# An attention and feed-forward block: V by seven products, K's and Q's weights together, codes by bits, norms on ScalarE

## Chip, cores and metric

The kernel runs on one core of a Trainium2 chip. The metric is the device time of one execution in microseconds. Times of before: 1510.03, 1510.06 and 1511.17 us, median 1510.06.

The engines are called PE (TensorE matmul), PEld (its weight loads), DVE (VectorE), ACT (ScalarE), POOL (GpSimd) and SP (SyncE, which issues all DMAs here).

## What is computed

16 sequences of 256 tokens, model width 256, 16 heads of 128, feed-forward width 2048. Everything is float32; the feed-forward weights come as 4-bit codes, two to a byte, with one scale for 32 of them.

```python
x = L0_attn_x                                    # (16, 256, 256)
n = layernorm(x)
q, k, v = (einsum('bpd,hde->bphe', n, W) + b for W, b in ((W_Q, b_Q), (W_K, b_K), (W_V, b_V)))
s = where(causal, einsum('bqhe,bkhe->bhqk', q, k) / sqrt(128), -1e5)
z = einsum('bkhe,bhqk->bqhe', v, softmax(s))
x = x + layernorm(einsum('bqhe,hed->bqd', z, W_O) + b_O)
n = layernorm(x).reshape(4096, 256)
Wg, Wu, Wd = (LUT[codes] * scales for each of gate, up, down)    # (2048,256), (2048,256), (256,2048)
x = x + layernorm((gelu(n @ Wg.T) * (n @ Wu.T)) @ Wd.T)
```

## The kernel before

**Three passes for a product.** Matmuls run on float32r operands. A matrix is kept as a high part (`hi`, rounded by a copy on ACT) and a rest (`lo = x - hi`, by a subtraction on DVE or POOL); `mm3` (L352) multiplies hi x hi, hi x lo and lo x hi into one PSUM bank. So a product of 128 x 128 by 128 x 512 is three matmuls, and what one operand costs elsewhere is an ACT copy and a subtraction.

**Attention.** The 4096 tokens are 8 blocks of 512 (two sequences). A unit is one head in one block, 128 units in all; a pair of heads shares the K, Q and output weights, a group of four heads (`w`, 32 groups) shares V's. The main loop (L1023) takes one step per unit and keeps several units in flight. In step `i` it records, in this order: scores and exps of unit i+4 (`st_s`, L421), K and Q of unit i+5 (`st_qk`, L370), the transpose of the probabilities on DVE (`st_t`), the output product of an earlier pair (`st_o`), the split of the turned probabilities (`st_p`), a quarter of V (`st_v`, L402), the product with V of unit i (`st_z`, L492), and the DMAs that write and read back the transposed probabilities through HBM (`hop`, `pt`: `st_w`, `st_b`), which land one and two steps before they are used.

`st_v` makes V for 128 tokens of each of the two sequences and 512 columns: two contraction halves (`kt`) x three passes = 6 matmuls of 512 columns into the bank `pv`; four such calls make a group. The first two are split into `vh` (ACT) and `vl` (DVE, from the bank), the last two are copied to `vr` (ACT), because the last 128 tokens of a sequence meet only the diagonal tile, which is multiplied unsplit in float32.

**Order.** Every engine works through its instructions in the order in which they are recorded; `run` (L95, so nearly all rows of the profile say L99) and `dma` (L86, rows say L91) enforce it. Side jobs are generators in lanes (`splits`, `urgent`, `behind`, `made`, `spare`, `idle`). Each `yield` names the engine of the job's next piece (V_ is DVE, G_ POOL, A_ ACT, N_ none), and `slot(kinds)` (L133), called at fixed places of a step, runs one piece of the first lane whose next piece has that kind.

**Weights.** In the first block `w_raw` (L283) loads raw weights, `w_split` (L297) splits them and `w_keep` writes hi and lo to HBM; from the second block on `w_get` (L331) loads these: K and Q 512 KB each for a pair, three steps before use, V 2 x 512 KB for a group. Each kind has two buffers.

**Norms.** `ln1` (L231) and `mid` (L555) compute means and variances on DVE, the power -1/2 on POOL, and apply them with `ln_apply` (L175) on POOL, four instructions of 128x256 for each norm; only the last block's `mid` does it on ACT (`ln_apply_act`, L183).

**Feed-forward weights.** From the end of the first block on, `f_make` (L618) decodes 24 pieces of codes on DVE: two extractions, a sign, a mask, and four operations that turn the code's three bits into a value with maxima; `f_scale` (L650) multiplies by the scale on POOL, splits, and builds four sums of 128x128 tiles for gate and up.

**Feed-forward.** Gate and up are already made by seven products in place of eight (`Two`, L778 on): with the token halves 11, 21, ... and the weights' sums, `m1` to `m7` are accumulated so that four results come out of seven products (the Winograd form of Strassen's method). `x_ops` (L710) makes the token sums.

Of the kernel before, what the change touches and what calls it, by code (L numbers as in the profile page):

```python
# [13 lines left out]
BF16 = mybir.dt.bfloat16  # L14
# [4 lines left out]
P = 128  # L19
# [9 lines left out]
def kernel(  # L29
# [21 lines left out]
    qscale = -1.0 / math.sqrt(E)  # L51

# [122 lines left out]
    def ln_apply(dst, src, mv, rs, t):  # L175
        run(nc.gpsimd.tensor_scalar, dst, src, mv[:, t, 0:1], rs[:, t : t + 1], ALU.subtract, ALU.mult)

# [37 lines left out]
    def split_tokens(key, hop):  # L215
        xr = wide("xr")
        dma(xr, hop)
        yield A_, 8
        xr = xr.rearrange("p a (m i) -> p m a i", m=8)
        xt = work.tile([P, 2, 2, TB], F32R, tag="xT", name="xT", bufs=4)  # L220
        for kt in range(2):
            src = xr[:, 4 * kt : 4 * kt + 4]
            hi, lo = (xt[:, h, kt, :].rearrange("p (t a i) -> p t a i", t=4, a=4) for h in range(2))
            run(nc.scalar.copy, hi, src)
            run(nc.gpsimd.tensor_tensor, lo, src, f(hi), ALU.subtract)
            if kt == 0:
                yield A_
        XT[key] = xt
        ready.add(key)

    def ln1(b):  # L231
        xs = [x_load(x, b, hf) for hf in range(2)]
        yield V_, 7
        mv, rs = yield from ln_stats([xs[hf][:, t, :] for hf in range(2) for t in range(2)])
        xn = wide("xn")
        for t in range(4):
            yield G_
            ln_apply(xn[:, t, :], xs[t // 2][:, t % 2, :], mv, rs, t)
        yield V_
        hop = dram.tile([P, 4, 2 * P], F32, tag="xhop", name="xhop", bufs=2)  # L240
        yield from turn_tokens(hop, xn)
        yield N_, 5
        yield from split_tokens((1, b), hop)
# [38 lines left out]

    def w_raw(g, n):  # L283
        src = {"q": wq, "k": wk, "v": wv, "o": wo}[n]
        raw = work.tile([P, 512], F32, tag="raw", name=f"raw{n}", bufs=6)
        dma(raw, src[g])
        RAW[g, n] = raw

    def w_tile(n):
        return wp.tile([P, 2, 1024 if n == "v" else 512], F32R, tag=f"w{n}", name=f"w{n}", bufs=2)  # L290
# [4 lines left out]
    HALF = {}  # L295

    def w_split(p, n):  # L297

        raw = RAW.pop((p, n)).rearrange("p (k c) -> p k c", k=2)
        key, done = p, True  # L300
        if n == "v":
            key, done = p // 2, p % 2
            w = HALF.pop(key) if done else w_tile(n)
            if not done:
                HALF[key] = w
            wv_ = w_view(w)[:, :, :, (p % 2) * 256 : (p % 2 + 1) * 256]
        else:
            w = w_tile(n)
            wv_ = w_view(w)
        c = qscale if n == "q" else 1.0  # L310
        run(nc.scalar.activation, wv_[:, 0], raw, AF.Copy, scale=c)
        if n in "vo" and (p, n) != (0, "v"):
            run(nc.gpsimd.tensor_tensor, wv_[:, 1], raw, f(wv_[:, 0]), ALU.subtract)
        else:
            run(nc.vector.scalar_tensor_tensor, wv_[:, 1], raw, c, f(wv_[:, 0]), ALU.mult, ALU.subtract)
        ahead = p + (2 if n == "v" else 1)
        if ahead < NG:
            w_raw(ahead, n)
        if done:
            W[key, n] = w_view(w)  # L320
            late.append((now[0] + 4, w_keep, (key, n, w)))

# [8 lines left out]
    def w_get(p, n):  # L331
# [3 lines left out]
        elif p < len(pairs):  # L335
            overdue(now[0] + 4)
            if n == "v":
                key, part = p // 2, p % 2
                w = HALF.pop(key) if part else w_tile(n)
                HALF[key] = w  # L340
                dma(f(w[:, part]), WD[key % (NG // 2), n][:, part])
                if part:
                    W[key, n] = w_view(HALF.pop(key))
# [57 lines left out]

    def st_v(k):  # L402
# [7 lines left out]
        if hf == 0:  # L410
            if bi == 0:
                V[w] = [
                    work.tile([P, 2, 4 * E], t, tag=n, name=n) for t, n in ((F32R, "vh"), (F32R, "vl"), (F32, "vr"))
                ]
# [140 lines left out]
    def mid(b, oT):  # L555
# [14 lines left out]
        if beside:  # L570
            yield V_
            nb = ln_shift(mv, rs, 4)
        for t in range(4):
            yield A_ if beside else G_
            if beside:
                ln_apply_act(cols4(att[:, t, :]), o[t], nb, rs, t)
            else:
                ln_apply(cols4(att[:, t, :]), o[t], mv, rs, t)
# [8 lines left out]
        if beside:  # L587
            yield V_
            nb = ln_shift(mv, rs, 4)
        xn = wide("xn")  # L590
        for t in range(4):
            yield A_ if beside else G_
            to, src = pairs_of_h(xn[:, t, :], True), pairs_of_h(xt[t], False)
            if beside:
                ln_apply_act(to, src, nb, rs, t)
            else:
                ln_apply(to, src, mv, rs, t)
# [20 lines left out]
    def f_make(g, n, then):  # L618


        pk, sc = LD.pop((g, n))

        def small_tile(dtype, name):
            return work.tile([P, 2, 256], dtype, tag="code", name=name, bufs=3)

        c = work.tile([P, 2, 256], I32, tag="raw", name="codes", bufs=6)
        sg, t = small_tile(BF16, "sg"), small_tile(BF16, "t")
        run(nc.vector.tensor_scalar, c[:, 0, :], pk, 15, None, ALU.bitwise_and)
        run(nc.vector.tensor_scalar, c[:, 1, :], pk, 4, 15, ALU.arith_shift_right, ALU.bitwise_and)
        yield V_  # L630
        if then:
            f_load(*then)
        run(nc.vector.tensor_scalar, sg, c, 8.0, -2.0, ALU.is_ge, ALU.mult)
        yield V_
        run(nc.vector.tensor_scalar, c, c, 7, None, ALU.bitwise_and)
        yield V_
        run(nc.vector.tensor_scalar, t, c, 2.0, 8.0, ALU.mult, ALU.subtract)
        yield V_
        while unscaled:
            step(made)  # L640
        v = small_tile(BF16, "v")
        run(nc.vector.scalar_tensor_tensor, v, c, 0.5, t, ALU.mult, ALU.max)
        yield V_
        run(nc.vector.scalar_tensor_tensor, v, c, 2.0, v, ALU.subtract, ALU.max)
        yield V_
        run(nc.vector.scalar_tensor_tensor, v, sg, 1.0, v, ALU.add, ALU.mult)
        unscaled.append((g, n))
        add(made, f_scale(g, n, v, sc), G_)

    def f_scale(g, n, v, sc):  # L650
        scb = sc.unsqueeze(1).to_broadcast([P, 2, 256])
        if n == "d":
            full = work.tile([P, 2, 256], F32, tag="raw", name="full", bufs=6)
            w = f_tile(n)
            run(nc.gpsimd.tensor_tensor, full, v, scb, ALU.mult)
            unscaled.remove((g, n))
            yield A_
            run(nc.scalar.copy, w[:, 0], full)
            run(nc.gpsimd.tensor_tensor, w[:, 1], full, f(w[:, 0]), ALU.subtract)
        else:  # L660

            full = work.tile([P, 8, P], F32, tag="eight", name="full", bufs=1)
            run(nc.gpsimd.tensor_tensor, full[:, 0:4].rearrange("p (k c) n -> p k (c n)", k=2), v, scb, ALU.mult)
            unscaled.remove((g, n))
            w = f_tile("u")
            yield A_
            run(nc.scalar.copy, w[:, 0, 0:4], full[:, 0:4])
            run(nc.gpsimd.tensor_tensor, w[:, 1, 0:4], full[:, 0:4], f(w[:, 0, 0:4]), ALU.subtract)
            yield G_
            a11, a21, a12, a22, s1, s2, s3, s4 = (full[:, m] for m in range(8))  # L670
            for o, l, r, op in (
                (s1, a21, a22, ALU.add), (s2, s1, a11, ALU.subtract), (s3, a11, a21, ALU.subtract),
                (s4, a12, s2, ALU.subtract),
            ):
                run(nc.gpsimd.tensor_tensor, o, l, r, op)
            yield A_
            run(nc.scalar.copy, w[:, 0, 4:8], full[:, 4:8])
            run(nc.gpsimd.tensor_tensor, w[:, 1, 4:8], full[:, 4:8], f(w[:, 0, 4:8]), ALU.subtract)
        late.append((now[0] + 4, f_keep, (g, n, w)))

    def f_tile(n):
        if n == "d":
            return wp.tile([P, 2, 2, 256], F32R, tag="fd", name="wd", bufs=2)
        if n == "g":
            return wp.tile([P, 2, 1024], F32R, tag="wv", name="wg", bufs=2).rearrange("p s (m c) -> p s m c", m=8)
        return wp.tile([P, 2, 8, P], F32R, tag="fs", name="wu", bufs=2)
# [5 lines left out]
    def f_get(k, n):  # L692

        sb, g = divmod(k, NG)
        if sb < NSB:
# [3 lines left out]
            w = f_tile(n)  # L699
# [8 lines left out]
    I = {}  # L708

    def x_ops(sb):  # L710
# [48 lines left out]
        w = w_tile("k")  # L759
        yield from put("t3", w[:, 0], w[:, 1], t3)  # L760
        w = w_tile("q")
        yield from put("22", w[:, 0], w[:, 1], x22)
# [15 lines left out]
    class Two:  # L778
# [25 lines left out]
        def done(self, c, bb, a, op, b, now_=True):  # L804
# [8 lines left out]
            else:  # L813
                todo.append((nc.vector.tensor_tensor, t, t, GE.pop((self.k, c, bb)), ALU.mult))
                tag, pool = (("vh", work), ("vl", work), ("vr", work), ("wo", wp))[2 * bb + c]
                i = pool.tile([P, 2, TB], F32R, tag=tag, name="inter", bufs=2)
# [38 lines left out]
    GE = {}  # L855
    GRP = {}
# [161 lines left out]
    def weights(*of):  # L1018
        for pn, n in of:
            if pn > {"o": -1, "v": 2}.get(n, 0):  # L1020
                w_get(pn, n)

    for i in range(-5, N + 2):  # L1023
# [16 lines left out]
        while after:  # L1040
            run(*after.popleft())
        slot(V_)
        if i + 5 < N:
            st_qk(i + 5)
        slot(V_, urgent, behind)
        slot(G_)
        slot(G_)
# [11 lines left out]
        if 0 <= i + 4 < N:  # L1059
            st_v(i + 4)  # L1060
        if 0 <= i < N:
# [7 lines left out]
        else:  # L1069
            weights((p + 4, "k"), (p + 4, "q"))  # L1070
# [100 lines left out]
```

## Time and profile before

| | |
|---|---|
| median of three executions | 1510.06 us |
| the profiled execution | 1510.8 us, its span 1508.6 us |
| granted TensorE clock | 0.999 |
| mean DMA rate | 270 GB/s, 407.54 MB |

The span runs from the first to the last instruction; 2.2 us lie around it. In the groups of instructions a line reads: line, engine, operation, out <- in by tile names, shape, count, then busy us, mean ns of one, and idle time of the engine before them with who ended it. These are the groups that the change touches most; a matmul's mean includes its way through the array, so matmuls overlap and their pitch is shorter:

```profile
L99 PE MATMUL pv<-wv,xT 128*128 128x512 f32 x768 | 194.9, 389 | 0.0
L99 DVE TENSOR_TENSOR vl<-pv,vh 128x512 fp32r<-128x512 f32 x64 | 43.9, 685 | 0.0
L99 ACT COPY vr<-pv 128x512 f32<-128x512 f32 x64 | 37.7, 589 | 64.4 <-PE pv L99 64.2
L99 POOL TENSOR_SCALAR xn<-xs,mv,rs 128x256 f32<-128x256 f32 x56 | 69.5, 1245 | 1.5
L99 POOL TENSOR_SCALAR att<-o,mv,rs 128x256 f32<-128x256 f32 x28 | 34.1, 1221 | 0.8
```

The stretches show, for a piece of the span, how long each engine was busy, the clock, the share of time in which the 16 DMA engines were busy (DMA share) and what they moved.

### The profile page before, as it was taken

The page shows a single profiled execution, that of the slowest core. Times are in us where ns is not written, and L with a number is a line of the kernel's source. Part 1 is how long each engine was busy: PE and PEld are TensorE (multiplying, and loading weights), DVE is VectorE, ACT ScalarE, POOL GpSimd, SP SyncE. Part 2 cuts the span into 40 slices and gives each one's busy share as a digit, 9 for nine tenths or more (in the row PEclk, how much of TensorE's full clock was granted, in tenths as well). Part 3 has the DMA queues.
Part 4 walks back from the last instruction along what each step waited for, and adds up shares of the span by engine and source line. Part 5 has one row for each costly group of instructions (what it writes and reads, how often), then busy time and mean ns, then how long its engine had stood idle before and what let it go on. Part 6 is the DMA issues. An engine that isn't in the chain of part 4 may idle for free.

```text
span 1508.6 us, 25609 instructions
## 1 busy us (share of the span) xinstructions
PE 1491.7 (99%) x7831; PEld 1279.9 (85%) x7831; DVE 1158.8 (77%) x3015; ACT 1037.0 (69%) x2614; POOL 722.0 (48%) x947
## 2 busy tenths in 40 slices
PE   8999999999999999999999999999999999999997
PEld 7888888888888888888888888887888888888886
DVE  6876777787777777778778777777787787787876
ACT  6887767767676677676777767675766665666665
POOL 3754569677777776866876876870000000000000
PEclk9999999999999999999999999999999999999999
DMA  8998899999999899899999999986657465655561
GB/s 294 338 326 253 263 303 310 293 309 315 287 299 309 280 333 319 269 312 306 290 289 317 297 323 312 305 275 234 223 184 279 171 246 198 249 182 201 218 235 57
DMA packets 200426, 407.54 MB, mean 270 GB/s; under 512 B 21473, under 2 KB 128481, under 8 KB 189537
## 3 DMA queue, kind: packets, MB, share of 16 engines
q1 hardware_dynamic: 200288, 405.91, 80.4%
q8 instruction: 62, 1.02, 0.3%
q14 instruction: 76, 0.61, 0.1%
HBM read 294.15 MB, written 111.67 MB: 269 GB/s over the span
## 4 chain that ended last, share of the span: by engine, by line
PE 91%; DMA 3%; DVE 3%; ACT 2%; issue 1%; POOL 0%; SPq 0%; POOLq 0%; DVEq 0%; ACTq 0%
PE pd L99 13%; PE pq L99 11%; PE pv L99 11%; PE pk L99 11%; PE po L99 11%; PE sc L99 9%; PE pz L99 9%; PE pa L99 8%; PE pf L99 5%; PE pe L99 2%; DVE sum L99 1%; DMA xr<-xhop 1%; DMA wu<-fu 1%; DMA hop<-tr 0%; ACT pr L99 0%
## 5 line engine op out<-in xcount | busy, mean ns | idle before, releaser
L99 POOL TENSOR_SCALAR pr<-pr,rc 128x128 f32<-128x128 f32 (+1 forms) x512 | 251.8, 509 | 163.7 <-DVE rc L99 163.5
L99 DVE CUSTOM_DVE_ANT_0 sc<-sc,mask 128x128 f32<-128x128 f32 (+1 forms) x512 | 180.7, 374 | 192.4 <-PE sc L99 183.7
L99 POOL TENSOR_TENSOR rs<-rs,mhalf 128x4 f32<-128x4 f32 (+1 forms) x35 | 34.5, 987 | 482.6 <-DVE rs L99 273.5
L99 ACT ACTIVATE pr<-sc,mn 128x128 f32<-128x128 f32 (+1 forms) x512 | 208.7, 419 | 74.2 <-DVE mn L99 71.1
L99 PE MATMUL pd<-inter,wd 128*128 128x512 f32 (+1 forms) x792 | 197.8, 385 | 1.4 <-ACT inter L99 1.0
L99 PE MATMUL pk<-xT,wk 128*128 128x512 f32 x768 | 195.4, 390 | 0.4 <-POOL xT L99 0.3
L99 PE MATMUL pq<-xT,wq 128*128 128x512 f32 x768 | 194.9, 389 | 0.0
L99 PE MATMUL pv<-wv,xT 128*128 128x512 f32 x768 | 194.9, 389 | 0.0
L99 PEld LDWEIGHTS pd<-inter,wd 128*128 128x128 f32 x792 | 145.0, 188 | 34.5 <-DVE inter L99 2.8
L99 POOL TENSOR_TENSOR pl<-pt,ph 128x512 fp32r<-128x512 f32 x124 | 159.8, 1289 | 23.0 <-ACT ph L99 20.7
L99 PEld LDWEIGHTS pq<-xT,wq 128*128 128x128 f32 x768 | 144.2, 188 | 30.0
L99 PEld LDWEIGHTS pv<-wv,xT 128*128 128x128 f32 x768 | 144.2, 188 | 29.9
L99 ACT COPY part<-pa 128x512 f32<-128x512 f32 x192 | 111.9, 586 | 68.1 <-PE pa L99 65.6
L99 PE MATMUL po<-zh,wo 128*128 128x512 f32 x512 | 157.7, 389 | 0.1
L99 PEld LDWEIGHTS pk<-xT,wk 128*128 128x128 f32 x768 | 136.1, 189 | 21.1 <-POOL xT L99 0.8
L99 ACT CAST inter<-sum 128x512 fp32r<-128x512 f32 x128 | 80.1, 626 | 88.0 <-DVE sum L99 88.0
L99 ACT ACTIVATE zh<-pz,bqk 128x512 fp32r<-128x512 f32 x128 | 88.1, 689 | 71.5 <-PE pz L99 71.5
L99 DVE TENSOR_TENSOR inter<-sum,inter 128x512 fp32r<-128x512 f32 x128 | 89.0, 695 | 56.9 <-ACT inter L99 56.0
L99 DVE STREAM_TRANSPOSE tr<-pr 128x768 f32<-128x768 f32 x128 | 123.4, 964 | 4.5 <-DMA hop<-tr 1.2
L99 PEld LDWEIGHTS po<-zh,wo 128*128 128x128 f32 x512 | 96.0, 188 | 20.3 <-ACT ph L99 0.5
L99 DVE SCALAR_TENSOR_TENSOR kl<-pk,bqk,kh 128x512 fp32r<-128x512 f32 x128 | 94.9, 742 | 17.8 <-ACT kr L99 16.8
L99 PE MATMUL sc<-kr,qr 128*128 128x128 f32 x512 | 99.6, 276 | 5.3 <-ACT qr L99 5.3
(150 smaller groups left out, 3719.8 us busy)
## 6 DMA issues: line engine op xcount, KB each, us to landing
hop<-tr SPq DMA_DIRECT2D x512, 96.0 KB
pt<-hop SPq DMA_DIRECT2D x128, 384.0 KB
wk<-wk SPq DMA_DIRECT2D x64, 512.0 KB
wq<-wq SPq DMA_DIRECT2D x64, 512.0 KB
wo<-wo SPq DMA_DIRECT2D x64, 512.0 KB
wu<-fu SPq DMA_DIRECT2D x32, 1024.0 KB
wg<-fg SPq DMA_DIRECT2D x32, 1024.0 KB
wv<-wv SPq DMA_DIRECT2D x56, 512.0 KB
```

Source lines behind the costliest of these rows:

```text
L99: ins = op(dst, *args, **kw)
```

## The change

- **V by seven products.** From the second block on, V of a group is seen as 2 x 2 blocks: tokens of the two sequences against contraction halves against 256-column halves. `st_v1` and `st_v2` take over from `st_v` and make seven products, each of 2 x 3 matmuls of 256 columns, at two places of a step; partial results are copied by ACT or added by DVE into a tile `vv`, all through the one bank `pv`. `v_split` then splits a finished quarter with an ACT copy and a POOL subtraction. The first block keeps `st_v`.
- **Sums for it.** `split_tokens` makes four sums of the block's tokens (POOL), split into a second `xT` tile; `v_sums` makes four sums of V's weights in the first block (POOL, ACT) and writes them beside hi and lo, so a group's weights are 2 x 896 KB.
- **K and Q together.** One tile `wkq`, kept and loaded by one DMA of 1024 KB for a pair. The first feed-forward operands that borrow such a tile wait until the last K and Q.
- **Codes by bits.** `f_make` puts the code's bits straight into float16 fields with shifts and masks: five DVE operations of 128x256; the scale is multiplied by 16384 to make up for the exponent.
- **Norms on ACT.** `ln_apply` goes; all norms but the first block's use `ln_apply_act`, two instructions to a slot.
- **Places.** V's raw weights, the feed-forward gate and down weights and some of the intermediate tiles share buffers with other names (`fs`, `wv`, `vv`); one `slot(G_)` of a step becomes `slot(G_ + A_)`.

```diff
+    TIMES = {
+        1: (0, 0, 0, 0), 2: (1, 0, 1, 0), 3: (6, 0, 1, 1), 4: (2, 1, 1, 0),
+        5: (3, 1, 0, 0), 6: (4, 1, 1, 1), 7: (5, 1, 0, 1),
+    }
+    def v_times(w, m, start):
+        at, summed, kt, bi = TIMES[m]
...
+        if start:
+            VB[0] = ps.tile([P, 2, 2 * E], F32, tag="pv", name="pv")
+        for hf in range(2):
+            tok = slice(bi * S + hf * P, bi * S + hf * P + P)
+            mm3(
+                VB[0][:, hf], [(lambda a: xt[:, a, kt, tok], lambda c: wt[:, c, at, :])],
+                start=start and hf == 0, shared=True,
+            )
...
+    def v_split(w, g, bi):
+        c = slice(g * 256, (g + 1) * 256)
+        vh, vl = (t[:, bi, c] for t in V[w][0:2])
+        run(nc.scalar.copy, vh, vv[:, v_first(g, bi)])
+        run(nc.gpsimd.tensor_tensor, vl, vv[:, v_first(g, bi)], f(vh), ALU.subtract)
+    def st_v1(k):
+        w, r = divmod(k, 4)
...
+        p = v_times(w, (2, 6, 5, 4)[r], r != 1)
+        if r < 2:
+            run(nc.scalar.copy, v_part(w, 0, r), p)
+        elif r == 2:
+            run(nc.vector.tensor_tensor, v_part(w, 1, 1), p, v_part(w, 1, 0), ALU.add)
+        else:
+            run(nc.vector.tensor_tensor, v_part(w, 1, 0), v_part(w, 1, 0), p, ALU.subtract)
+    def st_v2(k):
+        w, r = divmod(k, 4)
+        if r == 3:
+            return
+        p = v_times(w, (1, 7, 3)[r], r == 0)
+        if r == 1:
+            run(nc.scalar.copy, v_part(w, 1, 0), p)
+        else:
+            o = v_part(w, 0, r // 2)
+            run(nc.vector.tensor_tensor, o, p, o, ALU.add)
...
         while after:
             run(*after.popleft())
+        if 2 * NG <= i + 4 < N:
+            st_v1(i + 4)
         slot(V_)
         if i + 5 < N:
             st_qk(i + 5)
+        else:
+            finished.append(i)
+        st_v3(i + 4)
         slot(V_, urgent, behind)
         slot(G_)
-        slot(G_)
+        slot(G_ + A_)
...
-        if 0 <= i + 4 < N:
+        if 0 <= i + 4 < 2 * NG:
             st_v(i + 4)
+        elif 0 <= i + 4 < N:
+            st_v2(i + 4)
...
-            weights((p + 4, "k"), (p + 4, "q"))
+            weights((p + 4, "kq"))
```

The decoding, the load of the two weights and the norms:

```diff
+        run(nc.vector.tensor_scalar, low, pk, 255, 12, ALU.bitwise_and, ALU.logical_shift_left)
+        run(nc.vector.scalar_tensor_tensor, both, low, 12, low, ALU.logical_shift_left, ALU.bitwise_or)
+        run(nc.vector.tensor_scalar, low, both, 3, 0x0E000E00, ALU.logical_shift_right, ALU.bitwise_and)
+        run(nc.vector.scalar_tensor_tensor, low, both, signs, low, ALU.bitwise_and, ALU.bitwise_or)
+        run(nc.vector.tensor_scalar, sc, sc, 16384.0, None, ALU.mult)
...
+            elif n == "kq":
+                w = w_tile(n)
+                dma(f(w), WD[p % NG, n])
+                for m in range(2):
+                    W[p, n[m]] = w_view(w[:, m])
...
         for t in range(4):
-            yield G_
-            ln_apply(xn[:, t, :], xs[t // 2][:, t % 2, :], mv, rs, t)
+            if t % 2 == 0:
+                yield A_
+            ln_apply_act(xn[:, t, :], xs[t // 2][:, t % 2, :], nb, rs, t)
```

In the order of instructions that the two programs have, PE loses 672 pv matmuls of 512 columns and gains 1176 of 256; DMAs go from 1324 to 1268.

## The prediction

> **What bounds the kernel now.** I read the page's first part, then the engines' waits, then the table by stretches, then the timeline of one step.
>
> ```profile
> span 1508.6 us, 25609 instructions
> PE 1491.7 (99%) x7831; PEld 1279.9 (85%) x7831; DVE 1158.8 (77%) x3015; ACT 1037.0 (69%) x2614; POOL 722.0 (48%) x947
> ```
>
> PE is busy for 99% of the span. Its waits name ten microseconds in all, most of them in the first steps:
>
> ```profile
> PE sc L99 <- ACT qr L99: 5.3, 5, 1.9
> PE warm L99 <- POOL ident masks.py:199: 1.6, 1, 1.6
> PE pd L99 <- ACT inter L99: 1.0, 3, 0.4
> ```
>
> The table by stretches (busy us of PE, PEld, DVE, ACT, POOL, then clock, DMA share, GB/s) shows two stages, attention (first three lines) and the feed-forward part:
>
> ```profile
> 520.00:640.00 120.00, 120.00 (x683) 105.63 (x682) 91.39 (x284) 85.40 (x245) 87.67 (x115) 1.00 0.92 305
> 640.00:760.00 120.00, 120.00 (x679) 105.39 (x678) 94.29 (x283) 85.08 (x242) 84.19 (x109) 1.00 0.94 302
> 760.00:880.00 120.00, 120.00 (x687) 105.75 (x686) 92.01 (x286) 85.75 (x243) 90.21 (x118) 1.00 0.94 305
> 1060.00:1200.00 140.00, 140.00 (x618) 115.63 (x617) 111.95 (x203) 91.46 (x171) 3.39 (x3) 1.00 0.59 219
> ```
>
> In attention PE never pauses at full clock, DVE stands at 77%, ACT at 71%, POOL at 73%, and the DMA engines at 0.92 to 0.94. So a step is worth what it takes off PE, as long as the four others keep up.
>
> **V's products.** The chain in order of time prices a 512-column matmul; the timeline of PE prices a 256-column one (start, length, instruction):
>
> ```profile
> 603.22 1.36 PE pv L99 x6
> ```
> ```profile
> 604.41 0.28 PE L99 MATMUL pz<-ph,vh 128*128 128x256 f32 x1
> 604.53 0.28 PE L99 MATMUL pz<-ph,vl 128*128 128x256 f32 x1
> 604.64 0.28 PE L99 MATMUL pz<-pl,vh 128*128 128x256 f32 x1
> 604.77 0.39 PE L99 MATMUL pz<-pt,vr 128*128 128x128 f32 x2
> ...
> 605.57 0.39 PE L99 MATMUL sc<-kr,qr 128*128 128x128 f32 x2
> ```
>
> Lengths overlap; the pitch from start to start counts. Six wide ones take 1.36 us, 227 ns each. The narrow ones follow each other at 0.11 to 0.13 us; over all pz the records' median is 119 ns, most between 113 and 121. Each loads its own stationary tile in both cases (as many PEld as PE instructions).
>
> A group is four heads in one block. Before, its V takes 4 x 6 = 24 wide matmuls; now 7 products x 2 token halves x 3 passes = 42 narrow ones. Blocks 2 to 8 hold 28 groups: 672 x 0.2267 = 152.3 us go, 1176 x 0.119 = 139.9 us come, **-12.4 us**. With 113 ns it is -19.4, with 121 ns -10.0; I take 119, the row of the same shape in the same stream. The wide products alone would promise an eighth (19 us); the rest is lost because a narrow matmul costs more than half a wide one.
>
> A rule that speaks against this is in the Trainium skill, "TensorE: Matmul & The Clock Gate", section Back-to-back issue gap: weight loads keep short matmuls from being cheap, about 81 ns at 128 columns and 131 ns at 512. An estimate by a straight line between those is 98 ns at 256, and the change would then cost 1176 x 98 - 672 x 131 ns = 27 us more. The trace has 227 and 119 ns, a ratio of 0.52 where the rule's is 0.75; I go by the trace.
>
> **What DVE, ACT and POOL gain and lose.** From the groups by shape:
> - DVE: the old decoding goes (codes 48 x 331 and 24 x 422 ns, sg 474, t 433, v 714, 709 and 753, each x24: 98 us). Five 128x256 operations a piece come, between 0.3 (codes<-ld) and 0.45 us, 45 us in all. 56 vl at 685 ns go (-38), 112 sums from PSUM come at 687 ns, the row of sum<-pf (+77), nb +3. Net -11 us.
> - ACT: 84 norms at 606 ns (+51); vh and vr copies, 112 x 589 ns, go (-66); 84 PSUM copies come (+49); 112 vh copies of 128x256 lie between 370 ns (oT<-pd) and 622 (a 512 copy), I take 400 (+45); xT +9, V's weight sums +5. Net +93.
> - POOL: 84 norms at 1.24 us go (-104); 112 vl of 128x256, between 463 ns (128x128) and 1290 ns (128x512), on the line 0.74 (+83); tokens' sums and splits +39, V's weight sums +22. Net +40.
>
> A step lasts 7.77 us now (sc to sc in the timeline) and 7.66 with 12.4 us less over 112 steps. Of it ACT then holds 6.3, DVE 5.9, POOL 6.0 us: 83% at most. All this lies beside PE. It costs nothing on average; its cover is gone where one step is overfull. The written order has two steps a block in which POOL is asked for about 8 us, then one of 6.4: a backlog under 1 us. The norms go to ACT in pairs of 1.2 us, one place of them between zh and the next exps, where ACT idles 0.87 us: exps come 0.3 us late, and qr is done 2 us before PE asks for it.
>
> **Waits that are added.** All seven products share the one bank pv, and each waits until ACT or DVE has read it. Behind PE's wait stands everything PE has. Counting from the first sc matmul of a step, PE's own rows (sc 1.17, product 0.71, K and Q 2.72, output 1.36 us) want the bank again at 6.0 us, and by the next step's first product at 7.66 + 1.17 = 8.8. ACT's last exp ended at 3.4 in the step at 605.57, its copy then at 4.0; DVE's second reciprocal stood at 4.2, its sum then ends by 4.8. Both have a microsecond to spare for the first of these. For the second, two of the seven products follow a DVE sum that stands behind the transpose:
>
> ```profile
> 611.84 0.98 DVE L99 STREAM_TRANSPOSE tr<-pr 128x768 f32<-128x768 f32 x1
> 614.12 0.30 DVE L99 CUSTOM_DVE_ANT_0 sc<-sc,mask 128x128 f32<-128x128 f32 x1 [1.30 <-PE sc L99]
> ```
>
> The step began at 605.57, so the transpose ends at 7.3 and the sum at 7.9: 0.9 us to spare, and DVE idled 1.3 there. I put 1.5 us for single late steps (0 to 5). The sums of tokens are written out a step before their first use except in the second block: inside that.
>
> **Start.** In the first block the sums of V's weights (5.5 us of POOL a group, 22 us) enter steps where PE still waits for qr. POOL ran 53 of 80 us there (50 to 130 us). The third and fourth groups' raw weights wait on SP until the sums are written; behind them stand hop and pt, wanted two steps later. I take 1 us (0 to 3).
>
> **DMA.** V's weights grow from 2 x 512 to 2 x 896 KB a group, 22 MB in all; K and Q move the same bytes in half as many, twice as long rows. Bounds: at attention's 324 GB/s per full share (305/0.94) the extra 0.79 MB adds 2.4 us to a group of 30.6 us, share 1.03; if the longer rows move like the feed-forward stage's (219/0.59 = 370) K, Q and V together (3.1 MB a group, then 3.9) go from 9.7 to 10.6 us, share 0.98. The trace's packets say less: 8192 bytes took 313 ns on average between 520 and 900 us, 4096 bytes 196, which leaves 0.95. I take 0.95 to 0.98, hidden, since loads are asked for two to three steps ahead. The joined K and Q tile is freed when pq ends, not pk, 1.36 us later: hidden by the same.
>
> **Decoding, feed-forward.** The pieces' last POOL product moves from step 122 to 114 of 128; x_ops now holds back two operands until the last K and Q (2 x 0.6 us of ACT, 2 x 1.29 of POOL, asked for four steps later). The feed-forward stage has the same matmuls, and its shared tiles come free in the same places. The end of attention had 1.2 us of idle PE; 0, within 1 either way.
>
> **Sum.** -12.4 + 1.5 + 1.0 = -9.9 us on the profiled execution's 1510.8 us (span 1508.6 and 2.2 around it): 1500.9. It lies 0.7 over the median of 1510.06, so **1500**.
>
> **Rivals.**
> - *More is gained*: narrow matmuls in an unbroken row reach 113 ns: -19.4 + 2.5, 1493. For it: that is the pitch after a clean fp32 pass. Against: 119 and 121 follow at once.
> - *The bank eats it*: POOL's longer queue delays pr, pr delays the transpose, and DVE's sum is late by over 0.9 us in half of the steps. 56 such products at 0.2 us are 11 us: 1510. For: POOL's pr ended right at the transpose in the step shown. Against: DVE's spare 1.3 us.
> - *Slower, by DMA*: if attention's 0.94 is already the share at which loads start to queue, so that nothing above 324 GB/s is to be had, a group needs (305 x 31.1 us = 9.5 MB, + 0.8) 10.3 MB / 324 GB/s = 31.7 us instead of 31.1, and PE waits for weights: +0.6 x 28 = 17 us, 1527. It decides from a share of 1.0 on. Against: PE waited for no weights at 0.94, and 8192-byte rows are cheaper per byte.
> - *The change does not do what it says*: excluded; the built order has 1176 narrow pv matmuls in place of 672.
>
> **Chances.** Forecast (1496 to 1504) 0.62; more 0.08; bank 0.12; DMA 0.18. A difference under 0.2% (3 us) cannot be told from none in this kernel. Faster 0.70 (first two), same 0.12, slower 0.18. The range reaches to 1492 below, most of the gain at 113 ns, and to 1516 above, over the bank and into the DMA case.
>
> **What would show it.** Pitch of pv at 119 ns and PE busy near 1479 us: the main term. PE pv waiting for DVE vv or ACT vv: the bank. PE pv or pk waiting for DMA wv or wkq, with a share of 0.99: DMA. PE sc waiting for ACT qr after the first 60 us: ACT. I am wrong if narrow matmuls with their own weights do not keep 119 ns over six in a row, or if PE's waits in attention exceed some 6 us.

## The result, and the profile after

The changed kernel took **1527.7 us** (median of 4 runs, 1526.6 to 1533.8) against 1510.05 us (1509.5 to 1511.2) for the kernel before, run beside it: ratio 1.0125, 95% interval 1.0111 to 1.0139. It is slower, where the forecast was 1500. The profiled execution is the longest of the four, 1533.8 us with a span of 1532.0; what is read from it below is compared with the profiled execution of before (span 1508.6), 23.4 us apart, and the medians are 17.6 us apart.

The first part of the page, after:

```profile
span 1532.0 us, 26757 instructions
PE 1492.1 (97%) x8335; PEld 1299.4 (85%) x8335; DVE 1159.4 (76%) x3020; ACT 1111.7 (73%) x2804; POOL 726.9 (47%) x1041
```

PE has 504 instructions more, as the change says, and is busy as long as before instead of 12 us less. The longest waits of PE (us in total, times, longest):

```profile
PE pv L100 <- DVE vl L100: 9.2, 2, 7.3
PE pv L100 <- DVE vv L100: 7.4, 4, 2.5
PE sc L100 <- ACT qr L100: 6.0, 5, 2.3
PE pv L100 <- DMA wv<-wv: 2.6, 4, 1.0
```

The third was there before (5.3 us); the other three are new. They are few and long: one of 7.3 us, four of up to 2.5 us. The table by stretches, in the same stretches as before (busy us of PE, PEld, DVE, ACT, POOL, then clock, DMA share, GB/s):

```profile
520.00:640.00 120.00, 119.83 (x759) 108.43 (x758) 94.81 (x292) 96.09 (x271) 86.23 (x124) 1.00 0.97 332
640.00:760.00 120.00, 117.33 (x734) 105.52 (x733) 92.19 (x281) 92.92 (x262) 87.64 (x128) 1.00 0.96 329
760.00:880.00 120.00, 116.47 (x724) 104.86 (x723) 91.31 (x280) 92.76 (x260) 85.56 (x124) 0.99 0.97 325
1060.00:1200.00 140.00, 137.97 (x604) 112.61 (x603) 109.46 (x198) 87.39 (x162) 3.03 (x3) 1.00 0.59 216
```

In attention PE now has holes and DMA went from 0.92-0.94 to 0.96-0.97, at 325 to 332 GB/s instead of 302 to 305. DVE, ACT and POOL still stand below 0.82. A look at the average alone would not say where the time went; the lengths of the blocks do. They are taken from the trace, from the first sc matmul of one block to that of the next (us):

| kernel (profiled execution) | block 1 | 2 | 3 | 4 | 5 | 6 | 7 |
|---|---|---|---|---|---|---|---|
| before | 117.8 | 124.5 | 124.3 | 124.8 | 124.3 | 124.3 | 124.3 |
| changed | 132.7 | 124.1 | 123.0 | 127.2 | 123.4 | 126.4 | 128.7 |

The first block, which has no seven products at all, became 14.9 us longer. Blocks 2 to 7 became 6.3 us longer together, and they are of two kinds: one in which nothing goes wrong takes 123.0 us, 1.3 less than before, and the others are up to 5.7 us longer than that. The rest of the 23.4 us: start -0.3, last block with its end -0.4, the feed-forward stage +2.7.

**The first block.** SP's longest wait between 50 and 130 us (SPq is SP's queue of issues), then the longest of the other engines in the same stretch:

```profile
SPq L92 <- DMA wv<-rawv: 6.8, 1, 6.8
```
```profile
ACT wv L100 <- DMA rawv<-in_wv: 16.6, 2, 12.0
...
DVE vl L100 <- ACT vh L100: 12.3, 2, 9.5
PEld pv L100 <- DVE vl L100: 10.1, 2, 7.7
```

Read upwards from PE, in the lower lines: it waits for the bank pv, which DVE has not read (vl), as ACT has not copied it (vh), as ACT stands before the split of V's weights (wv), as the raw weights have not come. And the raw weights have not come since SP had not asked for them. SP's timeline shows that:

```profile
80.66 0.93 SPq L92 DMA_DIRECT2D wv<-rawv  x1
88.50 0.81 SPq L92 DMA_DIRECT2D rawv<-in_wv  x2
89.42 0.37 SPq L92 DMA_DIRECT2D pt<-hop  x1
89.84 0.42 SPq L92 DMA_DIRECT2D hop<-tr  x1
```

The write of the sums is issued at 80.66 us and lands 7.78 us later. The load behind it goes into the same buffer, so SP stands until 88.44, with pt and hop of the step behind it. The step of PE in which this falls lasts 17.86 us instead of 7.77. The same happens once earlier, with the third group's raw weights: the write of the first group's sums is issued at 39.28 us, SP waits 6.3 us for it and issues the load at 46.18, and the two steps of PE from 46.3 us on last 10.18 and 8.94 us where the kernel before has 6.41 and 7.77. These three steps make 15.0 us, the whole of the loss.

**A block with a stall.** The chain of waits of a stretch that ends at 500 us (start, length, piece; lines between left out):

```profile
469.20 9.01 DMA ohop<-oback
...
481.03 7.87 DMA o<-ohop
...
488.92 5.88 DMA hop<-tr
...
494.92 0.98 DVE tr L100
495.90 0.59 DVE vv L100
...
496.53 1.30 PE pv L100 x6
```

Three transfers of 128 KB, 512 KB and 96 KB each took 6 to 9 us (the page's median for hop<-tr is 4.4), and hop<-tr starts only when o<-ohop has landed, at 488.90 us, so the last two add up. DVE's transpose waited for the buffer tr until the hop before it had landed, the sum for pv stands behind the transpose, and PE waits for the sum. In DVE's timeline:

```profile
494.92 0.98 DVE L100 STREAM_TRANSPOSE tr<-pr 128x768 f32<-128x768 f32 x1 [2.98 <-DMA hop<-tr]
495.82 0.65 DVE L100 TENSOR_TENSOR vv<-pv,vv 128x512 f32<-128x512 f32 x1
```

The other two long waits of PE for vv, at 746 and 873 us, have the same chain: o<-ohop 7.26 and 8.94 us, then hop<-tr 6.70 and 5.83, then the transpose and the sum. The timeline of PE shows the price at 494 us:

```profile
496.53 1.30 PE L100 MATMUL pv<-wv,xT 128*128 128x256 f32 x6 [2.24 <-DVE vv L100]
497.63 2.76 PE L100 MATMUL pk<-xT,wkq 128*128 128x512 f32 x6
500.19 0.72 PE L100 MATMUL pq<-xT,wkq 128*128 128x512 f32 x2
```

PE loses 2.2 us to the wait. Then six pk matmuls take 2.56 us to the next one's start, 427 ns each instead of 227: the clock is halved from 497.0 to 500.4 us. The step lasts 11.97 us, 4.1 more than the 7.87 of an undisturbed one of its kind (of four steps three take 7.87 us and one 7.15; 7.69 is their mean).

### The profile page after: what moved, and what is told of

The parts are those of the page before. It is cut to its first block, busy times and chain, and to the rows that moved or that the text cites. A ratio compares the mean times of both kernels' runs of the same rounds, so it can differ in the third digit from the quotient of the medians.

```text
span 1532.0 us, 26757 instructions
## 1 busy us (share of the span) xinstructions
PE 1492.1 (97%) x8335; PEld 1299.4 (85%) x8335; DVE 1159.4 (76%) x3020; ACT 1111.7 (73%) x2804; POOL 726.9 (47%) x1041
## 4 chain that ended last, share of the span: by engine, by line
PE 75%; DMA 11%; DVE 4%; SPq 2%; ACT 2%; issue 1%; POOL 1%; POOLq 0%; DVEq 0%; ACTq 0%
PE pd L100 13%; PE pk L100 8%; PE po L100 8%; PE pq L100 8%; PE pa L100 8%; PE pv L100 8%; PE pz L100 7%; PE sc L100 7%; PE pf L100 5%; DMA ohop<-oback 2%; PE pe L100 2%; DMA hop<-tr 2%; SPq L92 2%; DMA o<-ohop 2%; DMA wv<-wv 1%; DVE sum L100 1%
## 5 line engine op out<-in xcount | busy, mean ns | idle before, releaser
L100 POOL TENSOR_SCALAR pr<-pr,rc 128x128 f32<-128x128 f32 (+1 forms) x512 | 217.6, 442 | 132.2 <-DVE rc L100 129.4
L100 PE MATMUL pv<-wv,xT 128*128 128x256 f32 (+1 forms) x1272 | 200.0, 293 | 19.3 <-DVE vl L100 9.2
L100 PEld LDWEIGHTS pv<-wv,xT 128*128 128x128 f32 x1272 | 179.0, 191 | 32.6 <-DVE vl L100 10.1
L100 PE MATMUL pk<-xT,wkq 128*128 128x512 f32 x768 | 200.6, 397 | 0.1
L100 PE MATMUL pq<-xT,wkq 128*128 128x512 f32 x768 | 195.4, 390 | 0.0
L100 PEld LDWEIGHTS pq<-xT,wkq 128*128 128x128 f32 x768 | 144.8, 189 | 30.9
L100 PEld LDWEIGHTS pk<-xT,wkq 128*128 128x128 f32 x768 | 137.5, 191 | 22.9 <-ACT xT L100 0.3
L100 PE MATMUL pd<-inter,wv 128*128 128x512 f32 (+1 forms) x594 | 152.0, 383 | 0.0
L100 POOL TENSOR_TENSOR vl<-vv,vh 128x256 fp32r<-128x256 f32 x112 | 83.5, 746 | 109.6 <-ACT vh L100 93.0
L100 PEld LDWEIGHTS pd<-inter,wv 128*128 128x128 f32 x594 | 109.4, 188 | 21.6
```

The costliest lines, as they stand in the source:

```text
L100: ins = op(dst, *args, **kw)
```

## Experiments

My theory after this reading: (A) the first block's loss is SP's wait behind the writing of the sums; (D) blocks 2 to 8 lose their gain to the seven products' bytes, which make transfers late now and then. The rivals: all of it is transfer rate (B), or POOL's and ACT's work on the sums (C), or the pv bank with DVE's queue (E), or one of the three other edits. Every kernel below was timed beside the kernel before on the same chip. Four chips were used in turn, on which the kernel before had medians of 1509.8 to 1510.5 us; differences between experiments are no finer than that.

### The sums from a second reading (a1_reload)

```diff
-            raw = RAWV[key][:, 2 * done : 2 * done + 2]
+            raw = RAW.pop((p, n)).rearrange("p (k c) -> p k c", k=2)
...
-        t = RAWV[key]
+        t = wp.tile([P, 8, 256], F32, tag="fs", name="rawv", bufs=2)
+        for part in range(2):
+            dma(t[:, 2 * part : 2 * part + 2].rearrange("p k c -> p (k c)"), wv[2 * key + part])
+        yield G_, 8
```

> The changed kernel, but in the first block V's raw weights come as in the kernel before (each group into a small tile of its own) and the sums are made later from a second reading of the raw weights, so that no transfer that the first block needs stands on SP behind the writing of the sums. It moves 1 MB more. Theory A (the first block's 14.9 us are SP held up behind the writing of the sums, with ACT, DVE and PE after it): the first block goes back from 132.7 to 118-120 us and the time to 1512-1515. Theory B (all of the loss is transfer rate, as in the rival of my prediction): no gain, 1526-1530. Theory C (the first block is late because POOL and ACT must make the sums, wherever their data come from): the first block stays above 128 us, 1523-1528.

Measured: 1518.12 us (12 runs, 1511.9 to 1525.7), ratio 1.0055 (1.0039 to 1.0072). The first block took 117.6 us. Theory A holds to the letter for that block: the same sums on the same engines, and all of the 14.9 us gone. The chain of waits from ACT's wv to PE's pv is absent from the stretch 50 to 130 us, and SP's wait at the writing of the sums is down from 6.8 to 2.2. B and C fall. But the time fell by 9.6 us only, so that it lies above the 1512 to 1515 us of theory A, and it now varies by 14 us from run to run: the stalls of the later blocks are still there (table below).

### Four of seven matrices loaded (a2_four_of_seven)

```diff
-                dma(f(w[:, part]), WD[key % (NG // 2), n][:, part])
+                dma(f(w[:, part, 0:4]), WD[key % (NG // 2), n][:, part, 0:4])
...
-                VB[0][:, hf], [(lambda a: xt[:, a, kt, tok], lambda c: wt[:, c, at, :])],
+                VB[0][:, hf], [(lambda a: xt[:, a, kt, tok], lambda c: wt[:, c, at % 4, :])],
```

> The changed kernel, but from the second block on only four of the seven matrices of V's weights are loaded (as many bytes as the kernel before moves) and the other three products take one of these four in their place, so V is another matrix; every instruction of the five engines stays. Theory A + D (the first block is SP's, and blocks 2 to 8 lose the gain to stalls that come from transfers at a share of 0.97): the first block stays at 132 us, the stalls of 9 to 12 us in blocks 5 to 8 go, blocks 2 to 7 fall from 752.8 to 738-742 us, the time to 1510-1517. Theory E (the shared pv bank and DVE's queue make these stalls, not transfers): blocks 2 to 7 stay at 750-753 us, 1525-1529. Theory B (all is transfer rate): 1498-1504.

Measured: 1518.34 us (1517.8 to 1518.6), ratio 1.0050 (1.0038 to 1.0062). Blocks 2 to 7 took 123.0 us each, six times, 738.0 in all, as theories A and D had it; the first stayed at 133.5, and the time lies a little above their 1510 to 1517. One of its stretches:

```profile
520.00:640.00 120.00, 120.00 (x765) 108.93 (x764) 95.24 (x288) 95.66 (x267) 85.64 (x125) 1.00 0.95 312
```

PE is full again with the same instructions on every engine, the same bank and the same queue of DVE; no wait of PE for DVE vv is left in the whole execution. So the bank is where the stall arrives, not what makes it: E falls. The spread of the time went from 7 us to 1 us. What the bytes do shows less in the share (0.94 to 0.96 in the three stretches from 520 to 880 us, 0.96 to 0.97 with all bytes) than in the rate: 310 to 314 against 325 to 332 GB/s.

### Both together (b1_reload_four)

This has the edits of the two before.

> The first block with the second reading of the raw weights, and from the second block on only four of the seven matrices of V's weights loaded (the other three products take one of these four, so V is another matrix); every instruction of the five engines stays. It is the seven products with neither of the two suspected costs. If the two are all of the loss and add up: 1518.3 less 14.9 of the first block, 1502-1505, with blocks 1 to 7 at 117.6 and six times 123.0 us. If the first block's delay only moves on: above 1508.

Measured: 1505.18 us (1504.4 to 1505.5), ratio 0.9966 (0.9954 to 0.9978). Its blocks: 117.7, then 125.0, four times 123.0, 123.4. The two causes together are all of the loss: with neither, the seven products' instructions take 4.6 us less than the kernel before (1509.82 beside it). Alone they gave 9.6 and 9.4 us, together 22.5. The 3.5 us by which that is more than the sum stay unexplained; single runs of the first kernel spread over 14 us. Block 2 took 125.0 us, with a wait of PE for qr of 1.7 us in it, where six blocks of 123.0 and 1502 to 1505 us were expected.

### All but the seven products (a3_eight)

```diff
-        if 2 * NG <= i + 4 < N:
-            st_v1(i + 4)
...
-        if 0 <= i + 4 < 2 * NG:
-            st_v(i + 4)
-        elif 0 <= i + 4 < N:
-            st_v2(i + 4)
+        if 0 <= i + 4 < N:
+            st_v(i + 4)
```

The weights' and the tokens' sums are left out with it, V's weights are again two transfers of 512 KB.

> The changed kernel with V made by eight products in all blocks, as before, without sums of V's weights or of the tokens; K's and Q's weights in one transfer, codes by bits and norms by ScalarE stay. If the other edits cost nothing, as I predicted: 1508-1512. If the norms on ScalarE or the joint transfer make the stalls of blocks 2 to 8: 1514-1520.

Measured: 1510.51 us (11 runs), ratio 1.0002 (0.9993 to 1.0011). The joint transfer, the decoding by bits and the norms on ScalarE cost and bring nothing that can be measured together. ACT's 40 us more (1077.0 us busy in this kernel) lie beside PE.

### The bytes without the products (b2_eight_bytes)

```diff
-                w = w[:, 0:2048].rearrange("p (s kc) -> p s kc", s=2)
+                w = w.rearrange("p (s kc) -> p s kc", s=2)
                 dma(f(w[:, part]), WD[key % (NG // 2), n][:, part])
                 if part:
-                    W[key, n] = w_view(w)
+                    W[key, n] = w_view(w[:, :, 0:1024])
```

It is a3_eight with V's weights stored and loaded as 2 x 896 KB.

> Eight products in all blocks and no sums, as in the kernel with the other three edits alone (1510.51), but V's weights are stored and loaded with 768 more columns in each half, which nothing reads: the bytes of the seven products without them. If bytes alone make the stalls of blocks 2 to 8: stalls of 9 to 12 us steps return in a block of two, 1518-1526. If the bytes only harm where PE waits for DVE's sums in the shared pv bank: 1510-1513.

Measured: 1516.96 us (1515.5 to 1521.0), ratio 1.0047 (1.0035 to 1.0059): 6.4 us more than without these bytes, for columns that nothing reads. Blocks of 126.2, 126.3 and 129.1 us stand beside undisturbed ones of 124.3. The time lies between the two ranges expected, nearer to the upper one, and the stalls are there: bytes alone make them. They reach PE by another way here:

```profile
PE pk L100 <- DMA wkq<-wkq: 6.7, 4, 2.9
```

In the chain to the longest of them, at 614 us, three transfers in a row take 7.3 to 8.0 us from issue to landing:

```profile
590.07 7.33 DMA pt<-hop
...
598.60 7.97 DMA xs<-in_x
...
606.59 7.52 DMA wkq<-wkq
```

Here K's and Q's weights themselves are late. What is late first differs from kernel to kernel; that something is late does not.

### K and Q in two transfers (a4_kq_two)

```diff
                 w = w_tile(n)
-                dma(f(w), WD[p % NG, n])
                 for m in range(2):
+                    dma(f(w[:, m]), WD[p % NG, n][:, m])
```

> The changed kernel, but K's and Q's weights come in two transfers of 512 KB into the two halves of the same tile. If the joint transfer is neutral: 1526-1530. If rows of 8 KB are what lets transfers keep up: slower, 1530-1536. If the joint transfer itself makes what stands behind it on SP late (SP waited 33.4 us at it, 14.0 at the two before): 1518-1524.

Measured: 1525.11 us (1519.3 to 1530.1), ratio 1.0091 (1.0071 to 1.0111). Its interval only touches that of the changed kernel (1.0111 to 1.0139), so two transfers may be worth some 2.5 us, but the runs spread over 11 us, and b4_balanced_kq, below, did not repeat it. It is inconclusive; rows of 8 KB are at least no clear help.

### The weights spread over the steps (b3_balanced, b4_balanced_kq)

```diff
-                dma(f(w[:, part]), WD[key % (NG // 2), n][:, part])
+                dma(f(w[:, part, 0:5]), WD[key % (NG // 2), n][:, part, 0:5])
+                REST.append((key, part, w))
...
             weights((p + 4, "kq"))
+            w_rest()
```

> The first block with the second reading of the raw weights, and V's weights spread over the steps: five of the seven matrices of a half behind Wo's in the odd step, two behind K's and Q's in the even one. Odd and even steps then load 1.18 and 1.31 MB instead of 1.44 and 1.05; all bytes stay. If the stalls come from the burst in the odd step, with the o and x loads of the block before on top: most of them go, 1504-1511. If it is the rate over the whole block that counts: 1515-1521, as with the second reading alone (1518.12).

> The same spread, with K's and Q's weights in two transfers of 512 KB. The kernel with two such transfers took 1525.11 where the changed one took 1527.70. If smaller transfers let the ones behind them through: 2 to 4 us below the spread alone. If not: the same as the spread alone.

Measured: 1517.2 us (1512.3 to 1517.4), ratio 1.0041 (1.0029 to 1.0053); with K and Q in two transfers 1520.75 us (1513.5 to 1526.0), ratio 1.0070 (1.0050 to 1.0090). The second reading alone had 1.0055. The spread is worth nothing that is clear of these intervals, and smaller transfers are not better on top of it. So the burst of wo, wv, o and x at once in the odd step, to which I had put the stalls down, is not most of what makes them.

### Fewer bytes: seven products in every second group (c1_alternate)

```diff
-        if 2 * NG <= i + 4 < N:
+        if 2 * NG <= i + 4 < N and (i + 4) // 4 % 2:
             st_v1(i + 4)
...
-        if 0 <= i + 4 < 2 * NG:
+        if 0 <= i + 4 < 2 * NG or 0 <= i + 4 < N and (i + 4) // 4 % 2 == 0:
             st_v(i + 4)
```

> The second reading in the first block, and seven products in every second group of V alone (eight in the others), so that half of the seven products' extra bytes are moved: 0.77 MB more than before for eight steps instead of 1.54. If stalls come only from transfers past some share, with half of the gain left on PE (seven blocks by 0.65 us): 1505-1509. If any more bytes than before bring stalls in proportion: half of the stalls with half of the gain, 1511-1515.

Measured: 1508.64 us (11 runs, 1506.5 to 1514.3), ratio 0.9990 (0.9982 to 0.9999). Blocks 2 to 7 took 123.6 or 123.8 us: half of the gain of 1.3, and no stall in them. That is the profiled execution (1509.55 us); the slowest of the 11 runs says that stalls may still come in others.

```profile
640.00:760.00 120.00, 120.00 (x725) 107.35 (x724) 90.85 (x280) 93.69 (x260) 82.24 (x117) 1.00 0.97 328
```

The expected range holds the time. It computes what the reference asks and is the fastest such kernel here, by a margin that its interval only just separates from none. Its share is 0.95 to 0.97 in attention, at 316 to 328 GB/s, and PE is full: neither figure alone tells a stretch with stalls from one without.

### Fewer bytes: Wo raw in every block (c2_wo_raw, c5_alt_wo, d1_wo_raw_later)

```diff
-                dma(f(w), WD[p % NG, n])
-                W[p, n] = w_view(w)
+                raw = wp.tile([P, 512], F32, tag="rawo", name="raww", bufs=1)
+                dma(raw, wo[p % NG])
+                late.append((now[0] + 6, o_split, (p, raw)))
```

> The second reading in the first block, seven products in all groups, and Wo's weights loaded raw in every block (256 KB instead of 512) and split in every block by ScalarE and GpSimd as the first block does, through a small tile of its own, for which the tiles of x go from four to three. Of the 192 KB that seven products add to a step 128 are saved, 64 remain; ScalarE has some 0.2 and GpSimd some 0.4 us more in a step. If the bytes make the stalls: most of them go, 1505-1511. If ScalarE and GpSimd have no room left in a step of 7.69 us: 1514 and above.

> Both of the two before: seven products in every second group and Wo's weights loaded raw. A step moves 32 KB less than in the kernel before the change. If the bytes make the stalls: none are left, and the time is that of half the gain, 1504.5-1507.5. If splitting Wo in every step costs by itself: 1509 and above.

Measured: 1562.38 us, ratio 1.0348 (1.0334 to 1.0362), and with every second group 1550.34 us, ratio 1.0264 (1.0250 to 1.0278). Both end in the open upper branch of what I expected, and far above its start. In the first one the share fell to 0.91 (140 to 880 us), and every block from the second on was stalled. ACT's waits between 260 and 520 us name a new cause, which is the edit's own:

```profile
ACT wo L100 <- DMA raww<-in_wo: 36.7, 15, 5.3
```

ACT stands before the split of weights that have not landed, and all that ACT does for PE stands behind it. The program puts the split six places, some 7.7 us, behind the transfer; in the trace SP issued the transfer only 2.7 to 5.5 us before ACT began the split (17 transfers of this stretch). With the split put later:

```diff
-                late.append((now[0] + 6, o_split, (p, raw)))
+                late.append((now[0] + 10, o_split, (p, raw)))
```

> The kernel with seven products, second reading and raw Wo once more, but the splitting of Wo stands ten places of the schedule (some 12.8 us) behind its transfer instead of six (7.7 us). The run before took 1562 us, and ScalarE waited for the raw weights in 15 of 17 steps of a stretch, 36.7 us in total, 5.3 us at most: a ScalarE that is held up, not too many bytes. If that wait is all of it: the wait goes below 5 us in the same stretch and the time to 1505-1511. If splitting Wo in every step is too much for ScalarE and GpSimd: above 1520 with no wait for the raw weights.

Measured: 1529.36 us, ratio 1.0120 (1.0104 to 1.0137): 33 us better, and still slow. In the same stretch:

```profile
ACT wo L100 <- DMA raww<-in_wo: 13.1, 6, 3.9
```

The wait is not gone, so neither side of the expectation was reached: it doesn't settle whether a Wo split in every step would fit beside the rest. Of the 12.8 us that the program leaves, the trace has 3.1 to 6.3 between SP's issue and the start of the split (17 transfers), and six of them still came too late, at a share of 0.92 (140 to 880 us): most of the distance is gone before SP comes to the transfer. Putting the split still later wasn't tried, and the other edit in these kernels, three tiles of x in place of four, wasn't tested by itself.

The blocks of the kernels that carry the verdicts (us):

| kernel | block 1 | 2 | 3 | 4 | 5 | 6 | 7 |
|---|---|---|---|---|---|---|---|
| a1_reload | 117.6 | 129.6 | 123.0 | 127.1 | 128.5 | 124.1 | 123.0 |
| a2_four_of_seven | 133.5 | 123.0 | 123.0 | 123.0 | 123.0 | 123.0 | 123.0 |
| b1_reload_four | 117.7 | 125.0 | 123.0 | 123.0 | 123.0 | 123.0 | 123.4 |
| a3_eight | 117.6 | 124.3 | 125.1 | 124.3 | 124.3 | 124.3 | 124.3 |
| b2_eight_bytes | 118.6 | 126.2 | 124.3 | 126.3 | 129.1 | 124.3 | 125.1 |
| b3_balanced | 117.8 | 128.0 | 123.0 | 123.4 | 124.9 | 123.0 | 124.1 |
| c1_alternate | 119.1 | 123.6 | 123.8 | 123.6 | 123.8 | 123.6 | 123.6 |

## Why the prediction was wrong

The forecast was 1500 in a range of 1492 to 1516, and the kernel took 1527.7. Two steps failed, by what the runs showed: the writing of the sums at the start, put at 1.0 us, cost 14.9; and the added bytes, put at nothing because DMA was to stay "hidden", cost 6.4 us by themselves (b2_eight_bytes) and 9.4 to 12.9 in the changed kernel. Step by step:

- **PE's products, -12.4: right in mechanism, a little too large.** The pitch of pv's narrow matmuls is 120 ns (median; 119 forecast). In an undisturbed block all pitches from a pv matmul to the next instruction add up to 19.95 us instead of 21.76: -1.81 a block, where 12.4 / 7 = 1.77 was forecast. What I had not costed stands in the next product: K's six matmuls, which come right behind pv's six narrow ones now, take 22.20 us a block instead of 21.76 (226.7 ns each before; 233, 236, 228, 233, 231 and 227 in their order now), and pz 18.65 instead of 18.56. That leaves 1.28 a block, 9.0 us over seven blocks.
- **Single late steps, +1.5 (0 to 5): too small, for the wrong reason.** I worked out DVE's 0.9 us to spare from one step of the kernel before, in which hop had landed in time. In the changed kernel PE did wait for DVE's sum (7.4 us, 4 times), but a2_four_of_seven removes every such wait without touching DVE, the bank or PE. In its trace the slack held in every step of blocks 2 to 7; that it rests on hop landing in time was not in the sum. The stalls cost 14.8 us in blocks 2 to 7.
- **Start, +1.0 (0 to 3): the largest miss.** The sentence names the mechanism (the third and fourth groups' raw weights wait on SP until the sums are written, with hop and pt behind them), and prices it with nothing worked out. The price was 14.9 us in the profiled execution, through two waits of SP of 6.3 and 6.8 us, and a1_reload takes all of it away. The working was at hand: a transfer of 1 MB takes microseconds to land, SP does nothing else meanwhile, and what PE needs is two steps behind. After has 9.5 us as the median from issue to landing of these very writes (wv<-rawv); the page of before, as I read it, had no time to landing, and I should have bounded it from below (1 MB at 305 GB/s is 3.4 us, with nothing ahead of it) instead of leaving it out.
- **The others, 0: right.** a3_eight at 1.0002 shows the norms, the joint transfer and the decoding at nothing together. The norms' two-step backlog in POOL and ACT's 93 us more did not reach PE. In the feed-forward stage (first pe matmul to the end) the trace has 487.4 us before, 489.0 in a3_eight and 490.0 in the changed kernel: some 1.6 us of the other edits, more than the 0, within 1, that I gave, and the medians do not show it.
- **DMA, hidden at 0.95 to 0.98: the share was right, "hidden" was not.** The measured share is 0.96 to 0.97. I took PE's lack of waits for weights at 0.94 as a sign that there is room up to 1.0. b2_eight_bytes shows 6.4 us lost to the bytes alone, at 0.96 to 0.97. So the point at which bytes begin to cost does not lie at 1.0. What moved is how late the late transfers are. The traces tell the landing of 56 or 64 of some 390 hop transfers between 140 and 900 us: the slowest tenth took 7.4 us or more in the changed kernel and 7.3 in b2_eight_bytes, against 6.1 in a2_four_of_seven and 5.9 in a3_eight, while the medians lie between 3.9 and 4.4 in all four. Slow transfers alone are no sign of loss: the slowest pt<-hop took 9.5 us in a2_four_of_seven and 10.0 in a3_eight, and in blocks 2 to 7 of these PE never waited longer than 0.6 us. What lands late just where little time is left makes the stall: hop in the changed kernel, K's and Q's weights in b2_eight_bytes.

**The rivals.** *Slower, by DMA* gave 1527, the measured time, and it is right only by half. Its place was wrong for the most part (PE was to wait for weights, and did so for 2.6 us in all; its three longest waits behind the first block come through hop, DVE's transpose and the bank), its point of decision was wrong (1.0), and its price fits by accident: the bytes cost 9.4 us (a2_four_of_seven against the changed kernel) to 12.9 us (b1_reload_four against a1_reload), and the first block, which that rival does not hold, the rest. *The bank eats it* described what the waits show, and would have sent me to the wrong engine: not POOL is late, but hop (DVE waited for it before all three of those sums). *More is gained* falls with the pitch of 120.

The profiled execution's 23.4 us close so: +14.9 in the first block; blocks 2 to 7 at an undisturbed 123.0 us, 8.5 below before's 746.5, and 14.8 of stalls above that; -0.4 in the last block, +2.7 in the feed-forward stage, -0.3 at the start. They make 23.2. The medians can't be split as finely, since stalls differ from run to run.

On the Trainium skill's rule from "TensorE: Matmul & The Clock Gate", section Back-to-back issue gap, that the forecast weighed: this trace's 120 to 227 ns is a ratio of 0.53, near the 0.52 I took and far from the 0.75 estimated from the rule's two figures. The measurement decides.

## What to carry to other kernels

Where DMA stands at 0.93 in a stage, as here, price added bytes as delay of the transfer that has the least time to spare, not as share alone (all of them cost 6 to 13 us, half of them nothing that shows); test it by loading the bytes without using them, which takes one edit. Before a transfer is put behind another one in the same buffer, ask who issues it and what stands behind it in that queue: the wait costs the landing of the first for everyone. And a wait of PE is to be followed past the engine it names: here DVE, twice, was only the last to hear of a late transfer.

## What the runs showed of the hardware

- **A wait can cost PE more than its length, depending on where it falls.** PE's gap of 2.24 us that ends at 496.53 us was followed by 3.41 us of half clock from 496.98 on (pitches of 213 and 427 ns instead of 120 and 227), so that the step lost 4.1 us. The gap of 2.19 us that ends at 747.88 us was followed by no half clock. The clock rows suggest why: the halvings at 53.24, 90.79, 496.98 and 875.86 us are 11, 119 and 111 times 3.413 us apart, a fixed grid. The first gap lies inside one stretch of this grid; a boundary at 746.15 us parts the second into 0.46 and 1.73 us. In the profiles of all fourteen kernels, PE was idle for 1.0 to 1.74 us in 61 such stretches at whole clock, and none was followed by half clock; it was idle for 1.94 us or more in 35, and every one was (of ten between these bounds, eight). The Trainium skill, "TensorE: Matmul & The Clock Gate", section What's actually happening, states a half-rate idle state that is entered after at least one idle window of about 3.4 us. The length agrees with this case; that the window need only be idle for somewhat more than its half is what these traces add.
- **K's wide matmuls got a little slower.** Behind pv's six narrow ones they took up to 236 ns instead of 227, in five of six places; the outputs' product, behind wide ones, kept 226.7. Narrow neighbours alone do not explain it: in the kernel before, K's product stood behind the narrow ones of pz and sc and kept 227 in all six places. The cause is open.
- **More bytes widen the spread.** Kernels that move the bytes of before in attention agreed within 1.2 us over five runs (a2_four_of_seven, b1_reload_four), 3.0 over eleven (a3_eight) and 3.2 over 23 (the kernel before, beside them); those with all bytes of the seven products varied by 5 to 14 us (changed kernel, a1_reload, a4_kq_two, b3_balanced, b4_balanced_kq).
